# A selective-scan and attention kernel on one core: order of the scan's products, engine of a strided copy, row groups of a projection, and the way of the scans' ends

## The chip, the core and the metric

The kernel runs on one NeuronCore of a Trainium2 chip. The metric is device time in microseconds (us) of one execution, given as the median of several runs. One execution is also recorded by the hardware profiler; what is read from views of the profile below comes from that one.

The engines go by these names: PE is TensorE, DVE is VectorE, ACT is ScalarE, POOL is GpSimd, SP is SyncE (it only issues DMAs here). Each engine works through its own instructions in the order in which they were written.

## The reference, cut to what matters

The input is four images of 64 x 64 tokens with 128 channels, in float32. Layer 0 normalises each image by groups and puts it through a Mamba block in three token orders (forward, backward, and sliced: token l goes to place (l mod 256) * 16 + l div 256). For each order, with 256 inner channels d and 16 states n:

```
x     = silu(causal_conv(in_proj x))             # 4 taps
dt_raw, B, C = x_proj_w @ x                      # 8, 16 and 16 rows
delta = softplus(dt_proj_w @ dt_raw + dt_bias)   # 256 rows
h[d,n,t] = exp(delta[d,t] * A[d,n]) * h[d,n,t-1] + delta[d,t] * x[d,t] * B[n,t]
y[d,t]   = sum over n of h[d,n,t] * C[n,t],  plus D[d] * x[d,t]
```

The three results are added, gated by silu(z), projected and added to the input. Layer 1 follows on the 4096 tokens of each image: a self-attention with 16 heads of 8 channels over all 4096 tokens, with a small feed-forward part, and then a layer of 64 experts, for each of which a gate picks eight of an image's tokens. The change lies in layer 0 alone.

## The kernel before

**Inputs.** The class `Inputs` makes, image by image, what the scans need. `norm(b)` loads the image, transposes it on PE and normalises it into the tile xn (128 channels x 4096 tokens). For each of three orders and four chunks of T = 1024 tokens, `of_chunk` runs a chain: the convolution on PE (L361), silu on ACT (u, L368), `x_proj` on PE (L375) into a PSUM bank whose rows are B (from row 0), C (from row 32) and dt_raw (from row 64), a copy of that to the tile xd on ACT (L378), the projection to delta on PE (L394, a contraction over 8 rows), softplus out of ACT functions (L399 to L410) and a sum on PE (L417), and on DVE delta (r, L422) and delta * x (L426). Delta, delta * x, x and the B and C rows go to DRAM by DMAs that POOL issues. `slices(b)` copies xn into the sliced order (the tile xs) with one copy on POOL (L305); the source of that copy is read with a stride of 256 tokens. Three PSUM banks serve this part; `bank` waits until one is free.

**Scans.** The class `Scans` goes through 384 steps an image: 3 orders, 4 chunks, 8 groups k of 32 channels, 4 steps j. One step holds 8 channels x 16 states, that is 16 channels x 8 states on 128 partitions, over 1024 tokens; steps j and j+1 share loads. In `of_image` the parts of a step are

- `load`: from DRAM, spread over the partitions, delta and du (delta * x), and at a chunk's first two steps the B and C rows (L469, L487), and once in four steps x (us, L492). SP issues these; for image 0 ACT issues du. Loads are issued two steps ahead (AHEAD).
- `exp`: ACT makes dA = exp(delta * A) (L501), one step ahead.
- `step`: on DVE the product dB = du * B (L510), the scan h (L513), which starts from the value that the chunk before ended with, and the product h * C (L515), written over dB. Between them a copy on POOL (L514) keeps the last column of h in the tile ends, from which the next chunk's scan starts.
- `total`: PE adds over the states (L521), for two steps at a time, four to five steps later.
- `out`: DVE adds D * x (L537), and POOL stores the result.

Tiles come from pools with few buffers: three for delta, four for du, two for dA, three for dB, two for h. An instruction that writes a tile waits until the readers of the tile that had the buffer are done.

**The order of the work.** Nothing is reordered: the order on each engine is that of the calls. Generators yield at certain points, and a `Pace` runs so many pieces of one beside the other. First come all inputs, 1.5 pieces of them to each piece of the scans of image 0 (two pieces to a step). Then comes `block.opening(0)`, the tokens of image 0 for the attention, with 0.15 pieces of image 1's scans to each of its own. Then `block.loop(b)`: for each of 1024 rounds PE makes scores (L866), ACT their exponentials (L871), PE the weighted sums (L880), and beside it run the scans of the next image and, after them, its opening; the last image's loop has no scans beside it. The experts come last.

Of the kernel before, what the change touches and what calls it, by code (L numbers as in the profile page):

```python
# [11 lines left out]
F32 = mybir.dt.float32  # L12
# [4 lines left out]
P = 128  # L17
C = 128
L = 4096
NT = L // P  # L20
DI = 256
NS = 16
R = 8
SLICES = 16
T = 1024
NC = L // T
NS2 = NS // 2
NB = DI // 8
B_ROW, C_ROW, DT_ROW, X_ROWS = 0, 32, 64, 72
H, D, FFN = 16, 8, 512  # L30
VW = 9
VPAD = 168
# [102 lines left out]
def scan_weights(nc, const, load, load_ps, ident, in_proj_w, out_proj_w, dirs):  # L135

    w_z = const["fill"].tile([P, DI], F32, name="w_z")
    w_out = const["all"].tile([P, 2, C], F32, name="w_out")
    w_in = load.tile([P, 4, C], F32, tag="w_in", name="raw_in")
    nc.sync.dma_start(out=w_in, in_=in_proj_w.rearrange("(k p) c -> p k c", p=P))  # L140
    ps = load_ps.tile([P, 512], F32, tag="ps", name="ps_in")
    for m in range(2):
        nc.tensor.transpose(ps[:, m * P : (m + 1) * P], w_in[:, 2 + m, :], ident)
    nc.vector.tensor_copy(w_z, ps[:, :DI])
    raw = load.tile([P, DI], F32, tag="raw", name="raw_out")
    nc.sync.dma_start(out=raw, in_=out_proj_w)
    ps = load_ps.tile([P, 512], F32, tag="ps", name="ps_out")
    for m in range(2):
        nc.tensor.transpose(ps[:, m * P : (m + 1) * P], raw[:, m * P : (m + 1) * P], ident)
    nc.vector.tensor_copy(w_out.rearrange("p m c -> p (m c)"), ps[:, :DI])  # L150
    ws = []
    for i, d in enumerate(dirs):
        w = {}
        raw = load.tile([R + 2 * NS, DI], F32, tag="raw", name=f"raw_x{i}")
        nc.sync.dma_start(out=raw, in_=d["x_proj_w"])
        w["x"] = const["fill"].tile([P, 2, X_ROWS], F32, name=f"w_x{i}")
        nc.gpsimd.memset(w["x"], 0.0)
        for m in range(2):
            ps = load_ps.tile([P, 512], F32, tag="ps", name=f"ps_x{i}_{m}")
            k = R + 2 * NS  # L160
            nc.tensor.transpose(ps[:, :k], raw[:, m * P : (m + 1) * P], ident[:k, :k])
            for row, at, n in ((DT_ROW, 0, R), (B_ROW, R, NS), (C_ROW, R + NS, NS)):
                nc.vector.tensor_copy(w["x"][:, m, row : row + n], ps[:, at : at + n])
        raw = load.tile([P, 2, X_ROWS], F32, tag="raw_dt", name=f"raw_dt{i}")
        nc.gpsimd.memset(raw, 0.0)
        nc.sync.dma_start(out=raw[:, :, DT_ROW:], in_=d["dt_proj_w"].rearrange("(m p) r -> p m r", p=P))
        w["dt"] = const["fill"].tile([X_ROWS, 2, P], F32, name=f"w_dt{i}")
        ps = load_ps.tile([P, 512], F32, tag="ps", name=f"ps_dt{i}")
        for m in range(2):
            nc.tensor.transpose(ps[:X_ROWS, m * P : (m + 1) * P], raw[:, m, :], ident)  # L170
        nc.vector.tensor_copy(w["dt"][DT_ROW:].rearrange("r m p -> r (m p)"), ps[DT_ROW:X_ROWS, :DI])
        for name in ("conv_b", "dt_proj_b"):
            w[name] = const["fill"].tile([P, 2], F32, name=f"{name}{i}")
            nc.scalar.dma_start(out=w[name], in_=d[name].rearrange("(m p) -> p m", p=P))

        w["D"] = const["all"].tile([P, DI // 32], F32, name=f"D{i}")
        for g in range(4):
            nc.scalar.dma_start(out=w["D"][32 * g : 32 * g + 32], in_=d["D"].rearrange("(k p) -> p k", p=32))

        taps = load.tile([P, 2, 4], F32, tag="taps", name=f"taps{i}")  # L180
        nc.scalar.dma_start(out=taps, in_=d["conv_w"].rearrange("(m p) k -> p m k", p=P))
        w["conv"] = const["fill"].tile([P, 4, DI], F32, name=f"conv{i}")
        for k in range(4):
            ps = load_ps.tile([P, 512], F32, tag="ps", name=f"ps_cv{i}_{k}")
            for m in range(2):
                cut = load.tile([P, C], F32, tag="cut", name=f"cut{i}_{k}_{m}")
                nc.vector.tensor_scalar_mul(cut, w_in[:, m, :], taps[:, m, k : k + 1])
                nc.tensor.transpose(ps[:, m * P : (m + 1) * P], cut, ident)
            nc.vector.tensor_copy(w["conv"][:, k, :], ps[:, :DI])
        ws.append(w)  # L190
    for i, (d, w) in enumerate(zip(dirs, ws)):

        w["A"] = const["all"].tile([P, 2, NB // 2], F32, name=f"A{i}")
        a_log = d["A_log"].rearrange("(k d) (q n) -> d q n k", d=16, n=NS2)
        for c in range(16):
            for q, by in enumerate((nc.scalar, nc.gpsimd)):
                by.dma_start(out=w["A"][c * NS2 : (c + 1) * NS2, q, :], in_=a_log[c, q])
    return w_z, w_out, ws


class Inputs:
# [98 lines left out]
    def slices(self, b):  # L300

        nc, xn = self.nc, self.normed[b]
        xs = self.big.tile([P, L + 3], F32, tag="xs", name=f"xs_{b}")
        nc.gpsimd.memset(xs[:, 0:3], 0.0)
        nc.gpsimd.tensor_copy(  # L305
            xs[:, 3:].rearrange("p (j i) -> p j i", i=SLICES),
            xn[:, 3 : L + 3].rearrange("p (i j) -> p j i", i=SLICES),
        )
        self.sliced[b] = xs
        yield  # L310

    def gate(self, b, g):
        nc, xn = self.nc, self.normed[b]
# [17 lines left out]
    def of_chunk(self, b, order, c):  # L331
        while b not in self.normed or (order == 2 and b not in self.sliced):
            yield WAIT
        src = self.sliced[b] if order == 2 else self.normed[b]
        nc, w, key = self.nc, self.ws[order], f"{b}_{order}_{c}"
# [18 lines left out]
        halves = [slice(g * 512, (g + 1) * 512) for g in range(T // 512)]  # L354
        u = self.piece.tile([P, 2, T], F32, tag="u", bufs=2, name=f"u_{key}")
        banks = []
        for m in range(2):
            ps = yield from self.bank(f"cv_{key}_{m}")
# [13 lines left out]
        ps = yield from self.bank(f"xd_{key}")  # L372
# [16 lines left out]
        r = self.piece.tile([P, 2, T], F32, tag="r", bufs=2, name=f"r_{key}")  # L389
        banks = []  # L390
        for m in range(2):
            ps = yield from self.bank(f"dt_{key}_{m}")
            for cut in halves:
                nc.tensor.matmul(ps[:, cut], w["dt"][DT_ROW:, m, :], xd[DT_ROW:, cut], start=True, stop=True)  # L394
            banks.append(ps)
        yield
        for m in range(2):
            bias = w["dt_proj_b"][:, m : m + 1]
# [13 lines left out]
        banks = []  # L412
# [19 lines left out]
class Scans:  # L432
# [23 lines left out]
    def of_image(self, b, made, alone=False):  # L456

        nc = self.nc
# [36 lines left out]
        def exp(s):  # L495
            order, c, k, j = steps[s]
            t = tiles["delta", s]
            if j % 2 == 0:
                tiles["delta", s] = self.deep.tile([P, T], F32, tag="dA", bufs=2, name=f"dA_{b}_{s}")
            A = self.ws[order]["A"][:, j % 2, 2 * k + j // 2].unsqueeze(1)  # L500
            nc.scalar.activation(tiles["delta", s], t, AF.Exp, scale=A)  # L501

        def step(s):
            order, c, k, j = steps[s]
            at = 4 * k + j
            dA, du = tiles.pop(("delta", s)), tiles["du", s]
            if j % 2 == 0:
                tiles["du", s] = self.deep.tile([P, T], F32, tag="dB", bufs=3, name=f"dB_{b}_{s}")
            dB = tiles["du", s]
            nc.vector.tensor_mul(dB, du, spread[order, c, "B", j % 2])  # L510
            h = self.deep.tile([P, T], F32, tag="h", bufs=2, name=f"h_{b}_{s}")
            first = 0.0 if c == 0 else ends[order, c - 1][:, at : at + 1]
            nc.vector.tensor_tensor_scan(h, dA, dB, first, ALU.mult, ALU.add)  # L513
            nc.gpsimd.tensor_copy(ends[order, c][:, at : at + 1], h[:, T - 1 :])  # L514
            nc.vector.tensor_mul(dB, h, spread[order, c, "C", j % 2])  # L515

        def total(s, y):
            order, c, k, j = steps[s]
# [45 lines left out]
        if b == 0:  # L564
            for w in self.ws:
                nc.scalar.activation(w["A"], w["A"], AF.Exp)
                nc.vector.tensor_scalar_mul(w["A"], w["A"], -1.0)
        exp(0)
        y = None

        def sums(s):
# [10 lines left out]
        for s in range(n):  # L582
            if s + self.AHEAD < n:
                yield from have(s + self.AHEAD)
            turn = s % 4 if s >= 4 else None
            if turn == 1:
                while not self.bank.free:
                    self.did.add("wait")
                    yield
                y = self.bank.grab(f"y_{b}_{s}")  # L590
            if s + self.AHEAD < n:
                load(s + self.AHEAD)
            if s + 1 < n:
                exp(s + 1)
                self.did.add("exp")
            if turn in (1, 2):
                sums(s)
                self.did.add("sum")
            yield
            step(s)  # L600
            if turn == 2 and not alone:
                finish(s - 3, y)
            if turn == 0 and alone and s >= 8:
                finish(s - 5, y)
            yield
            self.steps[b] += 1
# [878 lines left out]
```

## Time and profile before

| | us |
|---|---|
| median of three runs | 13118.68 (13114.79 to 13125.39) |
| the profiled execution | 13122.38 |
| its span, from the first instruction to the last | 13120.6 |
| PE busy in it | 12316.4 (94%) |
| ACT busy | 10692.1 (81%) |
| DVE busy | 8997.7 (69%) |
| POOL busy | 3486.8 (27%) |

A share of busy time is an average over the whole execution, and the stages differ: the inputs and the scans of image 0 fill the first sixth, the opening of image 0 takes some 240 us after that, the attention of four images fills most of the rest. In the lists of groups a row gives the line, the engine and operation, output and inputs by the program's names, the shapes, the number of instructions, then busy us and the mean ns of one, then the engine's idle time just ahead of them and what ended it. In a timeline a row gives start us, duration us, engine, line and operation. The durations of two instructions that follow each other on DVE overlap a little in the records.

### The profile page before, as it was taken

The numbers are of one execution on the slowest core, as the hardware profiler recorded it, in microseconds if no ns is written. First come the engines' busy times: TensorE is split into PE (matmuls) and PEld (weight loads), VectorE is DVE, ScalarE is ACT, GpSimd is POOL, SyncE is SP. The second block draws the span as 40 slices with busy tenths as digits, with TensorE's granted clock in tenths as the row PEclk, the third lists the DMA queues.
The fourth block names the chain that finished last, engine by engine and source line by source line (L and its number), as shares of the span: only waits on it lengthen the run. The fifth ranks groups of instructions, "written<-read, shape, count | busy, mean of one in ns | idle before, by whom it ended". The sixth has DMA issues, their size and how long they took to land. (4 is left out here: it accounts for less than half of the span.)

```text
span 13120.6 us, 214395 instructions
## 1 busy us (share of the span) xinstructions
PE 12316.4 (94%) x85447; PEld 3954.2 (30%) x85447; DVE 8997.7 (69%) x8649; ACT 10692.1 (81%) x10789; POOL 3486.8 (27%) x4200
## 2 busy tenths in 40 slices
PE   8898888399999999999999999999999999999995
PEld 3333333122222222233332222333222223333333
DVE  6999999788888877888888778888874211101122
ACT  5666666299999998999999989999998888888871
POOL 2333334222333322233333223333331000000000
PEclk8898888699999999999999999999999999999996
DMA  5666666644444445444444454444443100000004
GB/s 144 192 189 191 195 191 193 173 124 122 123 113 118 113 118 142 125 114 115 114 105 112 121 138 126 112 113 116 109 113 89 55 20 13 22 16 21 13 26 169
DMA packets 686549, 1482.22 MB, mean 113 GB/s; under 512 B 185054, under 2 KB 302374, under 8 KB 685286
## 3 DMA queue, kind: packets, MB, share of 16 engines
q1 hardware_dynamic: 494798, 1049.57, 31.0%
q0 software_dynamic: 139632, 300.84, 7.4%
q10 hardware_dynamic: 51112, 118.08, 3.4%
q8 instruction: 669, 10.96, 0.4%
q14 instruction: 338, 2.77, 0.1%
HBM read 1158.96 MB, written 308.94 MB: 112 GB/s over the span
## 5 line engine op out<-in xcount | busy, mean ns | idle before, releaser
L871 ACT ACTIVATE e<-s 128x1024 f32<-128x1024 f32 x8192 | 7908.9, 1028 | 1117.8 <-PE s L866 905.1
L866 PE MATMUL s<-qm,qT 32*128 32x512 f32 x32768 | 5441.0, 642 | 110.2 <-DMA qT<-d_q 58.9
L880 PE MATMUL acc<-e,v 128*32 128x512 f32 x32768 | 4388.1, 607 | 21.9 <-ACT av L889 19.6
L514 POOL COPY ends<-h 128x1 f32<-128x1 f32 x1536 | 1847.0, 1203 | 4876.5 <-DVE h L513 4869.2
L866 PEld LDWEIGHTS s<-qm,qT 32*128 32x128 f32 x32768 | 1796.7, 183 | 3197.0 <-issue 1416.5
L880 PEld LDWEIGHTS acc<-e,v 128*32 128x32 f32 x32768 | 647.0, 108 | 3160.9 <-issue 3024.1
L513 DVE TENSOR_TENSOR_SCAN h<-dA,ends,dB 128x1024 f32<-128x1024 f32 x576 | 1361.0, 2363 | 184.1 <-ACT dA L501 124.9
L513 DVE TENSOR_TENSOR_SCAN h<-delta,ends,du 128x1024 f32<-128x1024 f32 x576 | 1367.8, 2375 | 160.4 <-ACT delta L501 89.0
L510 DVE TENSOR_TENSOR dB<-du,B 128x1024 f32<-128x1024 f32 x768 | 935.4, 1218 | 190.3 <-PE y L521 182.8
L501 ACT ACTIVATE dA<-delta,A 128x1024 f32<-128x1024 f32 x768 | 888.5, 1157 | 156.9 <-DMA delta<-d_delta 150.8
L501 ACT ACTIVATE delta<-delta,A 128x1024 f32<-128x1024 f32 x768 | 887.8, 1156 | 151.3 <-PE y L521 140.5
L515 DVE TENSOR_TENSOR dB<-h,C 128x1024 f32<-128x1024 f32 x768 | 940.8, 1225 | 26.3
L515 DVE TENSOR_TENSOR du<-h,C 128x1024 f32<-128x1024 f32 x768 | 940.7, 1225 | 26.3
L510 DVE TENSOR_TENSOR du<-du,B 128x1024 f32<-128x1024 f32 x768 | 933.8, 1216 | 0.0
L895 POOL DMA_DIRECT2D d_ctx<-av x512 | 263.8, 524 | 1234.0 <-ACT av L889 1229.1
L361 PE MATMUL cv<-xn,conv 128*128 128x512 f32 x1024 | 511.8, 654 | 21.5 <-DVE xn L297 18.3
L521 PE MATMUL y<-du,sel 128*32 128x256 f32 x6144 | 492.5, 393 | 8.7 <-DVE du L515 8.7
L521 PE MATMUL y<-dB,sel 128*32 128x256 f32 x6144 | 497.3, 397 | 2.5 <-DVE dB L515 2.5
L513 DVE TENSOR_TENSOR_SCAN h<-dA,dB 128x1024 f32<-128x1024 f32 x192 | 446.9, 2328 | 52.7 <-ACT dA L501 32.6
L513 DVE TENSOR_TENSOR_SCAN h<-delta,du 128x1024 f32<-128x1024 f32 x192 | 440.1, 2292 | 38.4 <-ACT delta L501 14.4
L537 DVE SCALAR_TENSOR_TENSOR o<-us,D,y 128x256 f32<-128x256 f32 x384 | 205.9, 536 | 354.9 <-PE y L521 343.3
L550 POOL DMA_DIRECT2D d_y<-o x512 | 328.5, 669 | 276.3 <-DVE o L537 255.5
(252 smaller groups left out, 7609.2 us busy)
## 6 DMA issues: line engine op xcount, KB each, us to landing
delta<-d_delta SPq DMA_DIRECT2D x768, 512.0 KB
du<-d_du SPq DMA_DIRECT2D x576, 512.0 KB
du<-d_du ACTq DMA_DIRECT2D x192, 512.0 KB
d_u<-u POOLq DMA_DIRECT2D x48, 1024.0 KB, 5.6
B<-d_bc SPq DMA_DIRECT2D x96, 512.0 KB
C<-d_bc SPq DMA_DIRECT2D x96, 512.0 KB
d_delta<-r POOLq DMA_DIRECT2D x48, 1024.0 KB, 4.9
d_du<-u POOLq DMA_DIRECT2D x48, 1024.0 KB, 6.1
```

What stands on the lines that cost most here:

```text
L361: nc.tensor.matmul(ps[:, cut], w["conv"][:, k, m * P : (m + 1) * P], reads(k, g), start=(k == 0), stop=(k == 3))
L501: nc.scalar.activation(tiles["delta", s], t, AF.Exp, scale=A)
L510: nc.vector.tensor_mul(dB, du, spread[order, c, "B", j % 2])
L513: nc.vector.tensor_tensor_scan(h, dA, dB, first, ALU.mult, ALU.add)
L514: nc.gpsimd.tensor_copy(ends[order, c][:, at : at + 1], h[:, T - 1 :])
L515: nc.vector.tensor_mul(dB, h, spread[order, c, "C", j % 2])
L521: nc.tensor.matmul(y[32 * g : 32 * g + 32, : T // 4], self.sel[:, j // 2, :], hC[:, 256 * g : 256 * g + 256], start=(j == 0), stop=(j == 3),)
L550: nc.gpsimd.dma_start(out=to.rearrange("p (i j) -> p i j", i=SLICES)[:, :, at : at + n], in_=rows.rearrange("p (i j) -> p i j", i=SLICES),)
L866: nc.tensor.matmul(s_ps[:, k, :], qT[at : at + 32, kc * P : (kc + 1) * P], queries[j, qb][at : at + 32, :], start=True, stop=True,)
L871: nc.scalar.activation(e, s_ps, AF.Exp, scale=1.0 / math.sqrt(D))
L880: nc.tensor.matmul(accs[j, qb][32 * k : 32 * k + 32, :], v[:, kc, h * VW : h * VW + 32], es[i][k // 2][:, k % 2, :], start=(kc == 0), stop ...
L895: nc.gpsimd.dma_start(out=self.context[b][h * D : h * D + D, cut], in_=av[32 * k : 32 * k + D, :])
```

## The change

Four things are changed.

1. In a step of the scans, the product with B is made one step ahead: `inputs(s + 1)` stands between the scan of step s and its product with C. `inputs(0)` is called ahead of the first step.
2. The sliced copy moves from POOL to ACT and is cut in four pieces, with a yield after each.
3. The rows of `x_proj` are laid out anew: the eight dt_raw rows stand four times, at rows 0, 32, 64 and 96, with B at row 8 and C at row 40. The matrix of the projection to delta is likewise loaded four times. The four products of a chunk (two halves of the channels, two halves of the tokens) each use another group of rows, and both PSUM banks are taken ahead of the first of them.
4. The copy of a scan's last column into ends is made by a DMA on SP, issued in the step after the scan's, behind that step's loads. For the last chunk of an order, whose ends nobody reads, it is left out.

```diff
-B_ROW, C_ROW, DT_ROW, X_ROWS = 0, 32, 64, 72
+B_ROW, C_ROW, X_ROWS = 8, 40, 104
...
-            for row, at, n in ((DT_ROW, 0, R), (B_ROW, R, NS), (C_ROW, R + NS, NS)):
+            for row, at, n in [(32 * g, 0, R) for g in range(4)] + [(B_ROW, R, NS), (C_ROW, R + NS, NS)]:
                 nc.vector.tensor_copy(w["x"][:, m, row : row + n], ps[:, at : at + n])
...
-        nc.sync.dma_start(out=raw[:, :, DT_ROW:], in_=d["dt_proj_w"].rearrange("(m p) r -> p m r", p=P))
+        for g in range(4):
+            by = (nc.sync, nc.scalar)[g % 2]
+            by.dma_start(out=raw[:, :, 32 * g : 32 * g + R], in_=d["dt_proj_w"].rearrange("(m p) r -> p m r", p=P))
...
-        nc.gpsimd.tensor_copy(
-            xs[:, 3:].rearrange("p (j i) -> p j i", i=SLICES),
-            xn[:, 3 : L + 3].rearrange("p (i j) -> p j i", i=SLICES),
-        )
+        to = xs[:, 3:].rearrange("p (j i) -> p j i", i=SLICES)
+        src = xn[:, 3 : L + 3].rearrange("p (i j) -> p j i", i=SLICES)
+        n = L // SLICES // NC
+        for g in range(NC):
+            nc.scalar.copy(to[:, g * n : (g + 1) * n, :], src[:, g * n : (g + 1) * n, :])
+            yield
         self.sliced[b] = xs
-        yield
...
         for m in range(2):
-            ps = yield from self.bank(f"dt_{key}_{m}")
-            for cut in halves:
-                nc.tensor.matmul(ps[:, cut], w["dt"][DT_ROW:, m, :], xd[DT_ROW:, cut], start=True, stop=True)
-            banks.append(ps)
+            banks.append((yield from self.bank(f"dt_{key}_{m}")))
+        for m in range(2):
+            for g, cut in enumerate(halves):
+                at = 32 * (2 * m + g)
+                rows = slice(at, at + R)
+                nc.tensor.matmul(banks[m][:, cut], w["dt"][rows, m, :], xd[rows, cut], start=True, stop=True)
...
+        def inputs(s):
+            order, c, k, j = steps[s]
+            du = tiles["du", s]
+            if j % 2 == 0:
+                tiles["du", s] = self.deep.tile([P, T], F32, tag="dB", bufs=3, name=f"dB_{b}_{s}")
+            nc.vector.tensor_mul(tiles["du", s], du, spread[order, c, "B", j % 2])
+
         def step(s):
...
-            dA, du = tiles.pop(("delta", s)), tiles["du", s]
-            if j % 2 == 0:
-                tiles["du", s] = self.deep.tile([P, T], F32, tag="dB", bufs=3, name=f"dB_{b}_{s}")
-            dB = tiles["du", s]
-            nc.vector.tensor_mul(dB, du, spread[order, c, "B", j % 2])
+            dA, dB = tiles.pop(("delta", s)), tiles["du", s]
             h = self.deep.tile([P, T], F32, tag="h", bufs=2, name=f"h_{b}_{s}")
             first = 0.0 if c == 0 else ends[order, c - 1][:, at : at + 1]
             nc.vector.tensor_tensor_scan(h, dA, dB, first, ALU.mult, ALU.add)
-            nc.gpsimd.tensor_copy(ends[order, c][:, at : at + 1], h[:, T - 1 :])
+            tiles["h", s] = h
+            if s + 1 < n:
+                inputs(s + 1)
             nc.vector.tensor_mul(dB, h, spread[order, c, "C", j % 2])
+
+        def end(s):
+            order, c, k, j = steps[s]
+            at = 4 * k + j
+            h = tiles.pop(("h", s))
+            if c < NC - 1:
+                nc.sync.dma_start(out=ends[order, c][:, at : at + 1], in_=h[:, T - 1 :])
...
         exp(0)
+        inputs(0)
...
             if s + self.AHEAD < n:
                 load(s + self.AHEAD)
+            if s > 0:
+                end(s - 1)
             if s + 1 < n:
                 exp(s + 1)
```

More of the change, by code (lines that the diff above doesn't have):

```diff
@@ L170, in scan_weights @@
             nc.tensor.transpose(ps[:X_ROWS, m * P : (m + 1) * P], raw[:, m, :], ident)
-        nc.vector.tensor_copy(w["dt"][DT_ROW:].rearrange("r m p -> r (m p)"), ps[DT_ROW:X_ROWS, :DI])
+        nc.vector.tensor_copy(w["dt"].rearrange("r m p -> r (m p)"), ps[:X_ROWS, :DI])
         for name in ("conv_b", "dt_proj_b"):
```

## The prediction

> **What bounds the kernel now.** I read the stages first: the busy time of each engine in five stretches, cut at the first scan, at the last scan of image 0, at the first score matmul, at the start of the last image's tail and at its end. Columns: stretch, its length, then busy us (x instructions) of PE, weight loads, DVE, ACT, POOL, then granted TensorE clock, DMA share, GB/s.
>
> ```profile
> core 0: us, PE busy (x) PEld busy (x) DVE busy (x) ACT busy (x) POOL busy (x), PEclk, DMA share, GB/s
> 137.00:2363.00 2226.00, 1933.15 (x6631) 768.55 (x6631) 2114.05 (x1452) 1465.34 (x1176) 818.36 (x939) 0.88 0.66 192
> 2363.00:2602.00 239.00, 39.34 (x196) 30.51 (x193) 163.84 (x330) 25.53 (x21) 48.37 (x63) 0.54 0.57 159
> 2602.00:9870.00 7268.00, 7177.17 (x56170) 2129.18 (x56170) 6059.82 (x5300) 6709.35 (x6982) 2311.42 (x2665) 0.99 0.47 119
> 9870.00:12843.00 2973.00, 2934.08 (x21090) 889.11 (x21090) 557.53 (x1327) 2424.37 (x2530) 247.48 (x416) 0.99 0.11 31
> ```
>
> In the first stretch, the fill (all inputs and the scans of image 0), DVE is busy 2114 of 2226 us, and PE 1933, ACT 1465. In both attention stretches PE is busy 98.7%. So a change to the scans can pay in the fill alone; beside the attention loops it can only cost. Next, DVE's rows in the fill (busy us, mean ns | idle ahead) and its longest waits there:
>
> ```profile
> L513 DVE TENSOR_TENSOR_SCAN h<-delta,ends,du 128x1024 f32<-128x1024 f32 x144 | 352.2, 2446 | 29.6 <-ACT delta L501 11.0 <-DVE du L510 1.0
> L515 DVE TENSOR_TENSOR dB<-h,C 128x1024 f32<-128x1024 f32 x192 | 235.2, 1225 | 6.6
> L510 DVE TENSOR_TENSOR dB<-du,B 128x1024 f32<-128x1024 f32 x192 | 233.9, 1218 | 12.7 <-DMA du<-d_du 7.3 <-PE y L521 5.4
> ...
> DVE h L513 <- ACT dA L501: 17.7, 10, 3.2
> DVE h L513 <- ACT delta L501: 11.5, 7, 2.9
> ```
>
> DVE waits 29 us for exponentials and about 6 each for other things: it sets the fill. Last, the timeline of DVE (start us, duration), for what one step costs:
>
> ```profile
> 383.86 2.35 DVE L513 TENSOR_TENSOR_SCAN h<-dA,ends,dB 128x1024 f32<-128x1024 f32 x1
> 386.24 1.22 DVE L515 TENSOR_TENSOR dB<-h,C 128x1024 f32<-128x1024 f32 x1
> 387.39 0.47 DVE L537 SCALAR_TENSOR_TENSOR o<-us,D,y 128x256 f32<-128x256 f32 x1
> 387.78 1.22 DVE L510 TENSOR_TENSOR du<-du,B 128x1024 f32<-128x1024 f32 x1
> 389.13 9.21 DVE L513 TENSOR_TENSOR_SCAN h<-delta,ends,du 128x1024 f32<-128x1024 f32 x1
> ...
> 2347.71 2.35 DVE L513 TENSOR_TENSOR_SCAN h<-delta,ends,du 128x1024 f32<-128x1024 f32 x1
> 2349.98 0.65 DVE L665 COPY w<-ps_w 8x512 f32<-8x512 f32 x1
> 2350.56 1.20 DVE L515 TENSOR_TENSOR du<-h,C 128x1024 f32<-128x1024 f32 x1
> 2351.69 1.21 DVE L510 TENSOR_TENSOR dB<-du,B 128x1024 f32<-128x1024 f32 x1
> 2352.83 0.67 DVE L671 COPY w<-ps_w 128x512 f32<-128x512 f32 x1
> ```
>
> Two things are to be seen. From start to start, B to its scan takes 389.13 - 387.78 = 1.35 us and a scan to its C 386.24 - 383.86 = 2.38; both read what the one before wrote. Where a foreign copy happens to stand between (2347 to 2353), the same scan lets its follower start after 2.27 and the same B after 1.14. And the scan at 389.13 takes 9.21 us instead of 2.35: at 388.92 POOL begins the sliced copy (L305, four in all, 7.3 to 8.3 us).
>
> **What the Trainium skill says.** "VectorE: DVE Perf Modes", section "The DRAIN you can't avoid", states that the next op doesn't start until the pipe is empty and that a semaphore after each op costs nothing extra. This trace differs: the dependent pair is 0.21 us (B) and 0.11 us (scan) longer than the independent one, and I go by the trace. "GPSIMD Engine Reference", section "1. Specifications", says that GpSimd shares its SBUF interfaces with VectorE and contends with DVE instructions that have two SBUF inputs; the 9.21 us scan agrees. "DMA: Bandwidth & Descriptors", section "Anatomy of one DMA", gives a DMA a fixed cost of about 2.0 us (for the gpsimd path); used below as a lower end.
>
> **The change, part by part.**
>
> *C and the next B trade places.* Per step the DVE order becomes scan(s), B(s+1), C(s): no instruction follows its own producer any more. Step before 1.35 + 2.38 + 1.14 = 4.87 us, after 2.27 + 1.14 + 1.14 = 4.55: 0.32 us by 384 steps of image 0 = **-123 us**, all on DVE's path. The other 1152 steps lie beside attention, where PE hides it: 0. B(s+1) now comes 1.1 us earlier against its loads and against the PE sums that free its buffer; in the fill B waits only 12.7 us in all, so I leave that at nothing; in the loops B already waits there (182.8 us over the run, "dB L510 <- PE y L521") and C(s) queues behind it, but DVE has 1200 us of idle there.
>
> *The sliced copy goes from POOL to ScalarE in four pieces.* Each old copy lengthens one scan by 9.21 - 2.35 = 6.9 us: by four, **-27 us**. New on ACT: 16 copies, as long as the 128x1024 copy at L272 (about 1 us) or, as its source is strided, up to a quarter of POOL's (2 us): 16 to 32 us, hidden under ACT's 760 idle us in the fill. PE's 43.5 us of waits for xs become waits for ACT; PE isn't the bound there.
>
> *Four row groups for delta.* The four products (eight instruction records) of a chunk, 1.98 us to 3.78 us for each half of them in the timeline, could run side by side as the four row groups of the scores do (eight records per 1.14 us). That is up to 2.5 us by 48 chunks of PE time, off the path. Against it both banks must be free ahead of the first product, so the first half's two activations (2.2 us) start later. Net on the path between -20 and +10; I take 0. Setting up: 18 more tiny DVE copies (0.08 us each, DVE idle then), nine more DMAs, six of them on ACT ahead of its first copy at L272. ACT's issues there took 0.4 (2.79 us for 7) to 1.0 us (15.79 for 16): **+6** (2 to 15), as nothing covers ACT at the start.
>
> *The scans' ends go by DMA.* 1536 POOL copies (1.2 us each) go: DVE never waited for them, and C beside one takes 1225 ns against B's 1218, so at most -3 us. In their place 1152 DMAs on SP (none for a chunk that is the last). Each waits on SP for its scan, and everything behind it on SP waits too: the delta loads are issued one step later than now, still three steps (13 us) ahead of their scan; the us, B and C loads follow. SP's issue takes 0.5 us, and SP waits most of the fill (1209 us for scans), so its time is free. The new wait is this: h has two buffers, so scan(s+2) waits until the DMA has read end(s). From the end of scan(s) DVE has 1.14 + 1.14 + 2.27 + 1.14 + 1.14 = 6.8 us of other work. No such DMA is in the trace. Lower end 2.0 us (the page's fixed price) plus 0.5 of issue; nearest row above it, a 32 KB store from POOL in the fill (last column: us to landing):
>
> ```profile
> d_y<-o POOLq DMA_DIRECT2D x240, 32.0 KB, 3.7
> ```
>
> With its issue 4.2 us, and I take that: hidden, with 2.6 to spare. It isn't hidden where SP is held. (a) At the end of a chunk SP first waits for the C product of the chunk's step 30 before it may load the next C rows, then sends 512 KB ahead of the end: 2.3 + 0.7 of issue, then 0.5 and a landing of 5 (the 1 MB stores take 4.9 to 6.1): 8.5 against 6.8, 1.7 by nine boundaries = **+15** (0 to 45). (b) The x loads of three images hold SP until PE has transposed (17.5 us in all, longest 10): **+6** (0 to 25).
>
> *What is late next.* ACT's exponentials, 29 us of waits now; with DVE 7% faster, **+8** (0 to 40). In the stretch from 2363 to 2602 and at the loops' heads SP carries token loads, q stores and ends in one row; a store waiting behind an end costs **+6** (-5 to +40).
>
> Sum: -123 - 27 + 6 + 15 + 6 + 8 + 6 = -109. The profiled execution took 13122.4 us (span 13120.6 and 1.8 around it); less 109 is 13013. The median of the runs lies 3.7 below the profiled one: **13010 us**.
>
> **Rivals.** *PE takes over the fill.* PE is busy 1933 of 2226 us. Against: 58 us of its waits are for DVE's r, so they shrink with it, its granted clock was only 0.88, and delta's products shrink. For: it executes in a written order with ACT. If it can give up only a quarter of its 293 idle us, the fill gains 73 less the setup's 6: about 13050.
>
> *The ends become the bound (slower).* If an end lands L us after its scan, two steps take 2.27 + L once L is over 6.8, so the fill loses 288 x (L - 6.8) / 2. From L = 7.6 the whole gain of 109 is gone. At L = 9 it loses 317: about 13330. For it: a row of 512 KB loads in the same queue, and SP in order. Against: the delta load ahead of an end is issued a whole step (4.5 us) earlier.
>
> *SP's order costs the loops.* Ends hold up token loads and q stores where one image's opening is on the way; 33 us at each of three places (the opening, two loop heads) would take back 99: about 13110. Against it, PE waits only 27 us for o and 36 for e there now.
>
> *Not as it says:* row groups that don't run side by side would change nothing in the sum.
>
> **How the numbers follow.** Main case 0.62 at 13010 (its own range 12955 to 13065), PE's case 0.18 at 13050, the loops' case 0.12 around 13110, ends as the bound 0.08 at 13330. A measurement of this kernel tells about 0.2%, 26 us, from no change. Faster by more: all of the first two and a fifth of the third, 0.82; within: 0.08; slower: 0.10. The range for 8 in 10 is 12945 (all covers hold, delta's 20 as well) to 13100.
>
> **What would show it.** Right: in the fill, scan to B 2.27, B to C 1.14, C to scan 1.14; no scan over 3 us; the fill some 115 us shorter and DVE over 96% busy; loops within 10 us. Wrong: scans whose releaser is a DMA of ends, at every step and not only at chunks' ends; DVE in the fill waiting for y, sp or exp by over 100 us; idle PE at the loops' heads.

## The result, and the profile after

The changed kernel takes 13037.5 us (median of four runs, 13029.6 to 13044.7), the kernel before 13118.0 beside it: ratio 0.9938, 95% interval 0.992 to 0.9955. That is 80.5 us less; the forecast was 109 less. The profiled execution took 13034.6 us, its span 13032.8.

The stages of the kernel after: the fill and the opening cut nearly at the forecast's events (first product with B, just ahead of the first scan; last scan of image 0; first score matmul), then the attention of the first three images in one row, and all that follows in the fourth. Columns: stretch, length, busy us (instructions) of PE, weight loads, DVE, ACT, POOL, then granted clock, DMA share, GB/s.

```profile
135.00:2284.00 2149.00, 1795.93 (x6620) 715.01 (x6618) 2013.22 (x1441) 1491.32 (x1190) 337.80 (x546) 0.89 0.69 198
2284.00:2528.00 244.00, 41.38 (x206) 31.66 (x206) 166.72 (x343) 25.97 (x22) 37.39 (x57) 0.53 0.57 163
2528.00:10270.00 7742.00, 7647.65 (x59616) 2265.30 (x59616) 6051.66 (x5636) 7116.12 (x7404) 1042.31 (x1621) 0.99 0.46 116
10270.00:13032.00 2762.00, 2584.72 (x18788) 841.25 (x18788) 457.19 (x1141) 2044.98 (x2156) 205.52 (x361) 0.96 0.12 40
```

The kernel before, cut at the same four events, has 2223.8, 241.4, 7751.7 and 2766.9 us. So the fill gives 74 us of the 88 that the two profiled executions differ by, the loops 10, and nothing is lost at the opening but 2.5. The fill is where the forecast put the gain, but it had about 121 there.

The timeline of DVE in the kernel after (start us, duration) shows the new order:

```profile
385.65 2.35 DVE L522 TENSOR_TENSOR_SCAN h<-dA,ends,dB 128x1024 f32<-128x1024 f32 x1 [1.42 <-ACT dA L506]
387.92 1.20 DVE L513 TENSOR_TENSOR du<-du,B 128x1024 f32<-128x1024 f32 x1
389.04 1.22 DVE L526 TENSOR_TENSOR dB<-h,C 128x1024 f32<-128x1024 f32 x1
390.17 0.47 DVE L556 SCALAR_TENSOR_TENSOR o<-us,D,y 128x256 f32<-128x256 f32 x1
390.57 2.34 DVE L522 TENSOR_TENSOR_SCAN h<-delta,ends,du 128x1024 f32<-128x1024 f32 x1
```

From start to start, scan to B is 2.26 us, B to C 1.12, and C to what follows 1.13: 4.51 us a step (medians over the fill) where it was 4.88. The scan of 9.21 us that stood here before is 2.34 now, and no scan of the fill is over 2.6. Against that, the first line already shows a new wait: the scan stood 1.42 us for an exponential. The waits of DVE in the fill of the kernel after (total us, times, longest):

```profile
DVE h L522 <- ACT delta L506: 38.9, 18, 5.0
DVE h L522 <- ACT dA L506: 30.4, 21, 3.5
DVE h L522 <- DMA ends<-h: 26.4, 13, 5.5
DVE dB L513 <- PE y L540: 18.6, 9, 4.0
DVE dB L513 <- DMA du<-d_du: 12.0, 3, 7.7
```

Exponentials cost 69 us where the same view of the kernel before had 17.7 + 11.5 = 29; the ends, a wait that did not exist, 26; y 19 where it was 5. Steps and slow scans together give 0.366 x 384 + 27 = 168 us, and counted by the spacing of DVE's starts (how much later a start comes than in a pair that waits for nothing) the waits take 46 (exponentials), 27 (ends), 13 (y) and 5 (du) of it back. That leaves 77; waits for ACT's xn take 5 more and those for sp 2 less, and 74 are measured. The question for the runs is what makes the exponentials late, and what each of the four edits is worth by itself.

### The profile page after: what moved, and what is told of

The parts are those of the page before. It is cut to its first block, busy times and chain, and to the rows that moved or that the text cites. A ratio compares the mean times of both kernels' runs of the same rounds, so it can differ in the third digit from the quotient of the medians.

```text
span 13032.8 us, 214990 instructions
## 1 busy us (share of the span) xinstructions
PE 12155.9 (93%) x85447; PEld 3893.4 (30%) x85447; DVE 8719.1 (67%) x8667; ACT 10715.1 (82%) x10805; POOL 1660.6 (13%) x2660
## 5 line engine op out<-in xcount | busy, mean ns | idle before, releaser
L902 PE MATMUL acc<-e,v 128*32 128x512 f32 x32768 | 4385.4, 607 | 22.0 <-ACT av L911 19.5
L569 POOL DMA_DIRECT2D d_y<-o x512 | 328.4, 669 | 1987.7 <-DVE o L556 1870.6
L565 POOL DMA_DIRECT2D d_y<-o x512 | 254.3, 503 | 1892.5 <-DVE o L556 1881.3
L522 DVE TENSOR_TENSOR_SCAN h<-delta,du 128x1024 f32<-128x1024 f32 x192 | 438.6, 2284 | 56.8 <-ACT delta L506 48.0
L1033 DVE TENSOR_SCALAR h<-h,b 128x512 f32<-128x512 f32 x124 | 92.7, 748 | 400.1 <-PE s L888 400.0
```

What stands on the lines that cost most here:

```text
L565: nc.gpsimd.dma_start(out=to[:, end - T // 4 : end], in_=rows)
L569: nc.gpsimd.dma_start(out=to.rearrange("p (i j) -> p i j", i=SLICES)[:, :, at : at + n], in_=rows.rearrange("p (i j) -> p i j", i=SLICES),)
L902: nc.tensor.matmul(accs[j, qb][32 * k : 32 * k + 32, :], v[:, kc, h * VW : h * VW + 32], es[i][k // 2][:, k % 2, :], start=(kc == 0), stop ...
```

## The experiments

The first theory after the result was this: SP is held by the ends, the delta loads behind them are issued late, and so the exponentials come late. The rival: ACT cannot deliver them in time whatever SP does. Ratios below are to the kernel before, timed beside each experiment.

**All but the ends by DMA.**

```
-  h = tiles.pop(("h", s)); nc.sync.dma_start(out=ends[..], in_=h[:, T-1:])    # end(s), a step later
+  nc.gpsimd.tensor_copy(ends[order, c][:, at : at + 1], h[:, T - 1 :])         # right after the scan
```

> The changed kernel, but each scan's end is again copied by POOL, right after the scan. Theory (SP, held by the ends, issues the delta loads late, so exponentials come late, and the scans wait for the ends' DMA as well): in the fill the 27 us of waits for ends go and the waits for exponentials fall from 73 to about 30; the fill falls from 2149 to about 2080 and the whole to about 12970 us (12955 to 12990). Rival (the exponentials are late because DVE runs ahead faster or because ACT now makes the sliced copies): only the 27 us go, exponentials still cost 60 to 75, about 13010. Second rival (ends by DMA cost nothing net, since POOL's copies delay DVE as much): 13037.

Measured: 12998.0 us, ratio 0.9907 (0.9894 to 0.9921), about 39 less than with the ends' DMAs. The waits of DVE in its fill:

```profile
DVE h L521 <- ACT dA L506: 38.2, 23, 4.9
DVE dB L513 <- PE y L531: 22.1, 13, 3.9
DVE h L521 <- ACT delta L506: 20.7, 13, 4.9
DVE h L521 <- issue: 20.5, 8, 3.9
```

The ends' 26 us are gone, as both expected, but exponentials still take 59 us, and 79 if the row "issue", scans for which the profile names no releaser, is counted to them. My theory fell here. The loads are issued earlier: ACT's waits for delta's loads fall from 90 to 30 us, yet DVE gains nothing of it. The fill is only 18 us shorter than in the changed kernel (2131.3), and the loops 15 (7726.8 against 7741.8). So the ends cost more outside the fill than I had thought.

**The product with B a step ahead, alone** (the functions `step` and `inputs` of the diff, on the kernel before).

> Only the product with B is made a step ahead; ends and sliced copies stay on POOL, delta in one row group. Theory: the step falls by 0.366 us in 384 steps, -140 us, of which 10 to 25 come back as waits for exponentials and y: about 12995 us (12980 to 13010), four scans of 9 us remain. Rival (the faster DVE alone makes exponentials late by 45 us and PE by 13): about 13035.

Measured: 13031.0 us, ratio 0.9934 (0.9921 to 0.9946), the rival's value. By itself this edit makes the step 0.366 us shorter, 140 us in the fill, and its fill is 2164.3 us, only 60 less than before (three scans of over 9 us are left in it, not four):

```profile
DVE dB L508 <- PE y L526: 40.1, 19, 4.4
DVE h L516 <- ACT dA L501: 33.8, 18, 4.5
DVE h L516 <- issue: 16.7, 8, 4.3
DVE h L516 <- ACT delta L501: 13.6, 9, 3.4
```

With a faster DVE alone, 80 us of the 140 are lost again, with no end by DMA and no slice on ACT; by the spacing of DVE's starts 76 of them go to y and the exponentials (the row "issue" counted to these). What I had not expected: its loops are 20 us shorter (7731.1 against 7751.7). PE stands still for 86 us there where it was 102, above all because its waits for o (co at L980) are 15.6 us where they were 27.1; its busy time is 5 us less.

**The ends by DMA, alone** (`end(s)` and its call, on the kernel before).

> Only the ends go by DMA from SP; order of the products, sliced copies and delta's products as before. Theory (SP order): exponentials wait some 20 to 45 us more in the fill, scans wait 10 to 30 us for ends: 13150 to 13190 us. Rival (the late exponentials come from the faster DVE, so with the slower step nothing waits): 13115 to 13130.

Measured: 13144.1 us, ratio 1.0019 (1.0012 to 1.0026): slower by 23, just under the theory's range. In the fill the scans wait 19 us for ends and no longer for exponentials than before; the loops are 20 us longer (7771.5 against 7751.7). The fill is only 9 us longer (2233.0), since here B to scan takes 1.31 us where it was 1.35, some 16 us in 384 steps. So in the old order POOL's copy was not quite free for DVE. With the product ahead the three spacings are the same with the copy as with the DMA (2.26, 1.12 and 1.13 us in both).

**The sliced copy on ScalarE, alone.**

```
-  nc.gpsimd.tensor_copy(xs[:, 3:].rearrange(..), xn[:, 3:L+3].rearrange(..))
+  for g in range(NC): nc.scalar.copy(to[:, g*n:(g+1)*n, :], src[:, g*n:(g+1)*n, :]); yield
```

> Only the sliced copy goes to ScalarE in four pieces. Theory: no scan of 9 us is left, -27 us, ACT's 16 pieces of 1 to 2 us lie in its idle time: about 13091 us. Rival (the pieces hold up exponentials, 16 to 32 us of them): 13100 to 13120.

Measured: 13114.4 us, ratio 0.9996 (0.9988 to 1.0005): no difference that can be told, the rival's value. The row of the scans shows what it gives, and what it takes (busy us, mean ns | idle ahead):

```profile
L514 DVE TENSOR_TENSOR_SCAN h<-delta,ends,du 128x1024 f32<-128x1024 f32 x144 | 338.5, 2351 | 39.0 <-ACT delta L502 21.2 <-DVE du L511 0.5
L514 DVE TENSOR_TENSOR_SCAN h<-dA,ends,dB 128x1024 f32<-128x1024 f32 x144 | 338.5, 2351 | 35.5 <-ACT dA L502 17.8 <-DVE dB L511 0.5
```

The mean scan falls from 2446 and 2398 ns to 2351, but the waits for exponentials rise from 11.0 + 14.8 to 21.2 + 17.8 us, and those for sp and y by 5 and 3. The fill is 2223.0 us, as before.

**Four row groups, alone** (the diff's lines on `w["dt"]`, `X_ROWS` and the products).

> Only the four row groups for delta. Theory (in the kernel before, DVE waits 6 us for y and 7 for sp in the fill, and ACT 153 for dt, so there is little to win): 13105 to 13120 us. Rival (ACT's waits for dt are what makes exponentials late): the 29 us of waits for exponentials halve and the setup's 3 us is all that is added, 13090 to 13100.

Measured: 13108.6 us, ratio 0.9991 (0.9983 to 0.9999), 11 less, inside the theory's range. In 38 of the 48 chunks all four products start within 0.02 us of each other, and the chunk is done in 1.14 us where it took 3.67 or more; in the other ten the second pair waits for its bank, that is for DVE's r. Delta's products in the stretch from 137 to 2284 us, first of the kernel before, then of the changed one:

```profile
L394 PE MATMUL dt<-xds,w_dt 8*128 8x512 f32 x360 | 217.2, 750 | 70.4 <-DVE r L422 59.9 <-ACT xds L378 9.9
```

```profile
L400 PE MATMUL dt<-xds,w_dt 8*128 8x512 f32 x368 | 77.6, 713 | 85.8 <-DVE r L427 71.8 <-ACT xds L381 13.2
```

A part of what PE saves goes into waiting: with the row groups alone these products wait 120 us for r, where the kernel before has 60; this fits that both banks are now taken ahead of the first product.

**Product ahead with the sliced copy, and product ahead with the row groups** (ends on POOL in both).

> The product with B a step ahead and the sliced copy on ScalarE; ends on POOL and delta in one row group as before. Theory (row groups shorten PE's part of a chunk, so y comes earlier; without them y keeps DVE waiting some 40 us in the fill as with the product ahead alone, and ACT waits longer for dt): about 13018 us. Rival (the row groups carry nothing): 12998, as with the row groups.

> The product with B a step ahead and the four row groups; ends and sliced copy on POOL as before. Theory (ACT sets the pace of the exponentials, so the 32 us of sliced pieces on ACT give back what the four slow scans cost on DVE): 12995 to 13005, the same as with the copy on ScalarE. Rival (the sliced copy's 27 us are real): 13020 to 13028.

Measured: 13024.5 us, ratio 0.9929 (0.9916 to 0.9941), and **12992.4 us**, ratio 0.9901 (0.9888 to 0.9915). Both come out within 7 us of their theories and far from their rivals. The row groups take 39 us off the product ahead (13031.0 to 12992.4) and 26 off the pair with the slice (13024.5 to 12998.0): much more than the 11 alone. The sliced copy, on the other hand, makes no measurable difference once the row groups are there (12992.4 without it, 12998.0 with it). In the fill of the second kernel y costs 23.5 us where the product ahead alone had 40.1:

```profile
DVE h L520 <- ACT dA L505: 27.6, 17, 4.3
DVE dB L512 <- PE y L530: 23.5, 11, 4.9
DVE h L520 <- issue: 13.6, 5, 3.9
DVE h L520 <- ACT delta L505: 10.9, 8, 3.4
```

It is the best version of the study: ahead of the kernel before by 1%, and of the changed kernel by some 45 us.

**The ends' DMAs from POOL's queue.**

```
-  nc.sync.dma_start(out=ends[order, c][:, at : at + 1], in_=h[:, T - 1 :])
+  nc.gpsimd.dma_start(out=ends[order, c][:, at : at + 1], in_=h[:, T - 1 :])
```

> The changed kernel, with the ends' DMAs issued by POOL rather than SP. Theory (SP is held by the ends: the loads behind them come late): ACT's waits for delta's loads fall from 90 us to about 30 and the scans' waits for ends below 10, about 13000 to 13010 us. Rival (the DMA itself lands late beside the loads, whoever issues it): the scans still wait 20 to 40 us for ends, 13025 to 13045.

Measured: 13192.8 us, ratio 1.0053 (1.0039 to 1.0067), slower than either expectation. Its longest wait of DVE in the fill, and its row of DMA issues (last column: median us to landing):

```profile
DVE h L521 <- DMA ends<-h: 219.9, 82, 10.6
```

```profile
ends<-h POOLq DMA_DIRECT2D x1152, 0.5 KB, 3.9
```

The landing takes 3.9 us over the whole run and 4.6 in the fill (1.6 at the least, a tenth of them over 7.4), so by itself it is mostly within the 6.8 us that DVE has. In the fill half of these DMAs are issued within 0.9 us of their scan's end, but a quarter later than 4.4 us and the last at 11.3: POOL works in order too, and there the ends stand behind stores that wait for o, for r and for ACT. 4.4 + 4.6 is over the 6.8. Of the 220 us of waits, 173 lie behind the quarter that was issued over 4.4 us late, and 8 behind the half that was issued within 1 us.

**The end ahead of the loads on SP.**

```
-  if s + self.AHEAD < n: load(s + self.AHEAD)
-  if s > 0: end(s - 1)
+  if s > 0: end(s - 1)
+  if s + self.AHEAD < n: load(s + self.AHEAD)
```

> The changed kernel, but SP issues the end of step s-1 ahead of the loads for step s+2, not behind them. Theory (in the fill the ends wait only at a chunk's last two steps, behind the 512 KB load of C): the 27 us of scans' waits for ends fall below 5 and the whole to 13010 to 13020 us; the waits for exponentials stay near 70. Rival (the ends land late from the load of the DMA engines alone): 27 us stay, 13037.

> The changed kernel itself once more, on the chip of the runs beside it: 13037 us, within 10.

Measured: 13144.4 us, ratio 1.0022 (1.0013 to 1.0032), and for the changed kernel itself, once more, 13038.3. So this swap of two lines costs 106 us, where I had expected 20 to be won:

```profile
DVE h L522 <- ACT delta L506: 62.1, 29, 4.6
DVE h L522 <- ACT dA L506: 43.2, 23, 4.9
DVE dB L513 <- PE y L540: 42.3, 21, 4.1
...
DVE h L522 <- DMA ends<-h: 11.5, 7, 2.7
```

The ends' waits did fall, from 26 to 11.5, but the load behind an end now waits for that end's scan. From its issue to its scan a delta load in the fill has 26.5 us (median) in the kernel before, 24.7 with the ends on POOL, 19.5 in the changed kernel and 15.5 here; ACT's waits for delta's loads are 46, 30, 90 and 235 us. In the changed kernel most of the loss of lead is still covered; here it isn't. ACT works in order, so what stands behind a waiting exponential comes late as well; that y and sp wait longer (42 and 14 us) fits this, but was not tried by itself.

**No switch of ACT's table for the logarithm.** This kernel leaves out softplus's logarithm.

```
-  nc.scalar.activation(ln, e, AF.Ln, bias=1.0)
+  nc.scalar.activation(ln, e, AF.Identity, bias=1.0)
```

> The changed kernel with the logarithm of delta's chunks replaced by a plain pass (1 + e in place of log(1 + e), so delta is another number): as many ACT instructions, but the switch of the activation table to the logarithm and back falls away. Theory (exponentials are late because each stands behind bursts on ACT with table loads of 1.28 us between): the waits for exponentials in the fill fall from 73 to 30 to 45 us, the fill by 25 to 45, the whole to 12990 to 13015 us. Rival (exponentials are late because their loads are): 70 us of waits stay, 13030 to 13037.

Measured: 12995.5 us, ratio 0.9907 (0.9893 to 0.9921), 43 less than the changed kernel beside it. Exponentials cost 20.9 + 16.1 = 37 us in the fill where it was 69, the ends 27.5 as before, and the fill is 2112.4 us, 37 to 39 shorter:

```profile
DVE h L522 <- DMA ends<-h: 27.5, 12, 4.7
DVE h L522 <- ACT delta L506: 20.9, 15, 4.2
...
DVE h L522 <- ACT dA L506: 16.1, 17, 2.2
```

The pass in the logarithm's place takes as long (1.89 us against 1.91), so what goes is 82 table loads, 105 us of ACT's work. ACT's waits for delta's loads are even longer here, 111 us where the changed kernel has 90, so the loads are not what made most of the exponentials late. This is what a late exponential looks like in the timeline of ACT in the changed kernel:

```profile
523.91 1.13 ACT L506 ACTIVATE delta<-delta,A 128x1024 f32<-128x1024 f32 x1
525.06 1.28 ACT L415 ACT_TABLE_LOAD   x1
526.35 1.91 ACT L415 ACTIVATE ln<-e 128x2048 f32<-128x2048 f32 x1
526.42 0.52 ACTq L492 DMA_DIRECT2D du<-d_du  x1
528.28 1.28 ACT L328 ACT_TABLE_LOAD   x1
529.58 1.02 ACT L328 ACTIVATE z<-z 128x1024 f32<-128x1024 f32 x1
530.62 1.28 ACT L506 ACT_TABLE_LOAD   x1
531.91 1.15 ACT L506 ACTIVATE dA<-delta,A 128x1024 f32<-128x1024 f32 x1
```

```profile
528.46 1.22 DVE L526 TENSOR_TENSOR du<-h,C 128x1024 f32<-128x1024 f32 x1
533.10 2.35 DVE L522 TENSOR_TENSOR_SCAN h<-dA,ends,dB 128x1024 f32<-128x1024 f32 x1 [3.42 <-ACT dA L506]
```

Between two exponentials ACT works 6.9 us without a pause: a logarithm, a z and three table loads. A step of DVE is 4.5 us, so the scan stands 3.42 us. It is so nearly every time: of the 39 waits for exponentials in the fill of the changed kernel, 36 (62 of the 69 us) end behind a stretch of 7 to 28 us in which ACT never paused for more than 0.15 us, and 35 of these stretches began when PE delivered xd or dt. The run takes work from ACT and shortens these stretches at once; it does not tell the two apart. The Trainium skill, "ScalarE: Activation LUTs", section "What ACT_TABLE_LOAD costs", gives 1283 ns for a load, as here, and 1380 ns more for a drain; in this trace the next instruction starts within 0.02 us, so the longer price doesn't apply. In the fill of the changed kernel there are 238 such loads, 305 us of ACT's time.

## Why the prediction was right or wrong

**Right: the side, the place, and what a step gains.** The gain lies in the fill, the opening is within 2.5 us, and the three shorter spacings came as read from the foreign copies in the trace before: 4.51 us a step where 4.55 was worked out, -140 us where -123 stood. B itself is a little shorter too (1.20 us where it was 1.22); why is not shown. The forecast held the longer spacing of a dependent pair against the Trainium skill, "VectorE: DVE Perf Modes", section "The DRAIN you can't avoid"; that section adds that a next instruction which isn't held starts earlier, so the shorter spacings do not speak against it. The slow scans went (-27). The 512-byte DMA lands in 3.9 us over the run and 4.6 in the fill where it was recorded, on POOL's queue; 4.2 was taken (its 3.7 already counts from the start of the issue, so the 0.5 on top is counted twice). The shortest took 1.6, less than the 2.0 that served as the lower end.

**Only in part right: the total.** 13037 lies within the range, and nearer to the 13050 of the rival "PE takes over the fill" than to 13010. Of the forecast's own signs, a fill some 115 us shorter and a DVE over 96% busy did not come (74 us and 94%), and DVE's waits for y, sp and exponentials are 92 us, just under the 100 that were to show it wrong. It came this near with some luck: gains beyond the forecast made up for more than half of what the waits cost beyond it.

**The step that failed: "What is late next", +8 for exponentials, and nothing for y.** They cost +46, outside the 0 to 40 given, and +13, and these two terms are more than the whole miss. I took the waits of before and let them grow a little with DVE's pace. But ACT's work comes in bursts, and the slack of a burst is not the stage's idle time: a shorter step shows bursts that the longer one had covered. For ACT the 36 of 39 waits above show it; for PE, which makes y, it is inferred. The product ahead alone has 40 us for y and 64 for exponentials (the "issue" row included). My rival of PE taking over, with 13050 us, came near the 13031 of that single edit; but PE was only half of it, and in the whole change the row groups removed much of that half.

**The sliced copy: "hidden under ACT's 760 idle us" was wrong.** A piece takes 1.97 us (31.5 us for 16), the upper of the two ends I had given. The edit alone moved nothing, so what left DVE came back as waits for ACT and PE.

**The row groups: 0 was too little.** Alone they gave 11 us, inside the -20 to +10; together with the product ahead 26 to 39, outside it. "Off the path" held, nearly, for the kernel before; for the kernel with a faster DVE it didn't, and I had costed this edit against the former.

**"Beside the attention loops it can only cost" was wrong.** The product ahead alone makes the loops 20 us shorter, and the changed kernel keeps 10 of it, because PE waits less for DVE's o.

**The ends: the mechanism was right, the size too small.** The waits sit where step (a) put them: of the fill's 26.4 us the scans of step 31 carry 18.0 and those of step 0 of the next chunk 7.5, waiting for the ends of steps 29 and 30 behind the load of C. They cost 27 by spacing where +15 stood for (a) and +6 for (b). Step (b), SP held by the x loads until PE has transposed, is not seen: these waits of SP, 17.5 us in the fill of the kernel before, are gone from the fill of the changed one, and the delays that I found at the scans are at the chunks' ends. No run tried it by itself. In the loops +6 was forecast for the opening and the heads together; with the ends on POOL the loops are 15 us shorter, and the ends alone make them 20 longer. In all this edit costs 39 us: without it the change is at 12998. Of the 15, 9 are waits of PE (5 of them for o, 20.3 against 15.5 us) and 6 are busy time of PE; what lengthens that was not tried.

**Setup: +6 (2 to 15) was too much.** ACT's first copy of xn ends 2.8 us later (45.93 to 48.76 us), but the first scan starts at 136.2 us where it started at 138.1, and at 132.7 in the kernel with the slice alone, whose setup is the old one. What of it reaches the fill is less than this scatter.

**The rival of the ends as the bound** did not happen on SP, where only 13 scans of the fill waited for an end, but it is real: from POOL's queue the same DMAs cost 220 us of waits. What decided was less the landing than what stands ahead of the DMA in its queue.

The misses partly cancelled. Against the sum, by the two profiled executions, the step was 17 better than forecast, the opening and the loops together 13, the start 8 and the part after the loops 4; exponentials were 38 worse, y 13, the ends 6, and the loads of du and the wait for xn 5 each. That is 25 too slow; the two executions differ by 88 where 109 stood, 21 too little, and the few us between are small terms. (By the medians it is 80.5 where 109 stood.)

## What to carry to other kernels

When the engine that sets a stage gets faster, cost its suppliers by their longest uninterrupted burst against its new step, not by their idle share: here an ACT 69% busy was already too late 39 times, 36 of them behind such a burst. Cost each edit against the kernel that the others make, since the row groups were worth 11 us before and 26 to 39 after DVE's step had shrunk. And a small DMA costs what its queue makes it wait for, and what it makes wait behind it: the same 512 bytes cost 39 us on SP behind the loads, about 145 ahead of them, and 195 on POOL, against a POOL copy that leaves the spacings of the new order as they are.

## What the runs showed of the hardware that was not expected

- A table load stands on both sides of the logarithm: one ahead of each `ln` (47 in the fill of the changed kernel), and mostly another right behind it. Without the logarithm 82 of the fill's 238 loads are gone.
- A copy on ACT of 128x1024 elements takes 1.97 us where its source is strided by 256 elements (xs from xn), and 1.01 us where it isn't (xn from xt). The second source is PSUM and the first SBUF; which of the two makes the difference was not tried.
- Delta's products over eight rows start within 0.02 us of each other where they lie in different row groups: in 34 of the 48 chunks of the changed kernel all four, done in 1.14 us. In 13 of the other 14 the second half waits for DVE's r (2.78 us in one of them).
